# Turning x1 with VectorE block transposes and DMAs in place of TensorE transposes, in a two-layer graph kernel

## The chip, the cores and the metric

The kernel runs on one core of a Trainium2 chip. The metric is the device time of one execution in microseconds (us). Before the change the median of three runs is 2922.5 us (2921.11 to 2922.8). The profile is of one execution with a span of 2918.8 us.

Five engines work beside each other: TensorE (PE in the profile, with its weight loads as PEld), VectorE (DVE), ScalarE (ACT), GpSimd (POOL) and SyncE (SP), which here only issues DMAs. Each takes its own instructions in the order in which they stand. An instruction that has to wait for a semaphore holds up all that stand behind it on its engine.

## The reference

There are 64 graphs of 256 nodes with 512 features. The first layer is three graph convolutions with a residual and a layer norm; the second weighs a value projection with a softmax over the nodes. Cut to what matters:

```python
def gcn(x, adj, W, b):                      # per graph: [256,256] @ ([256,512] @ [512,512])
    return adj @ (x @ W) + b

h  = relu(gcn(x, adj, W1, b1))
h  = relu(gcn(h, adj, W2, b2))
x1 = layernorm(x + gcn(h, adj, W3, b3))     # "r" in the kernel

q, k = split(x1 @ Wqk)
v    = x1 @ Wv
agg  = adj @ (k * mask)
w    = mask / sqrt(512) * sum(q * agg, axis=-1)      # one score per node
out  = layernorm(x1 + softmax(w, over nodes) * v)
```

The kernel folds Wq and Wk into one matrix M once, so that the score is (x1 M) . (adj (mask x1)). All data are float32.

## The kernel before

Graphs go in pairs: 32 pairs, G = 2 graphs each. Every large product is a 2 by 2 block product by Strassen's scheme in Winograd's form: seven block products, numbered 1 to 7, in place of eight. For that, sums of blocks of both operands are made first. `a_sums` makes four sums `S` of the left operand and `b_sums` four sums `T` of the right one; `adj_sums` makes four sums `aS` of the adjacency. In the loop all three run on GpSimd.

```python
def padd(o, a, b, op=OP.add):
    nc.gpsimd.tensor_tensor(o, a, b, op=op)

def seven(mm, shape, c11, c12, c21, c22, plus=None):
    x = bank(shape); mm(1, x, True)             # left block (0,0)
    t1 = shaped(shape); nc.scalar.copy(t1, x)
    ...
    v = bank(shape); mm(7, v, True)             # needs S[2]
    mm(6, x, False)                             # needs S[1]
    u = shaped(shape); nc.scalar.copy(u, x)
    ...
    y = bank(shape); mm(2, y, True); c11(y, t1) # left block (0,1)
    mm(5, x, False)                             # needs S[0]
    q = shaped(shape); nc.scalar.copy(q, x)
    ...
    c22(v, q)                                   # reads the bank v ...
    mm(3, x, False); c12(x)                     # needs S[3]
    mm(4, v, False); c21(v, u)                  # ... that product 4 then adds to

def a_sums(hT):
    S = [pool.tile([P, 2, G, P], FP, name="S", tag="S", bufs=6) for _ in range(4)]
    blk = lambda h, k: hT[k][:, :, :, h * P:(h + 1) * P]
    padd(S[2], blk(0, 0), blk(1, 0), sub)
    padd(S[0], blk(1, 0), blk(1, 1))
    padd(S[1], S[0], blk(0, 0), sub)
    padd(S[3], blk(0, 1), S[1], sub)
    ...
```

Two generators run interleaved: `front(i)` computes the two hidden layers of pair i, and `back(i-1)` the rest of the pair before. In `back`, the third convolution ends in `r` (that is x1 before its layer norm). Then:

```python
    r = pool.tile([P, G, NH, D], FP, name="r", bufs=2)          # nodes on the partitions
    yield from adj_times(aS, C, ...)                            # writes r
    for g in range(G):
        layernorm(r[:, g])
    yield 8
    x1T = [pool.tile([P, 2, G, N], FP, name="x1T", tag="act", bufs=5) for _ in range(2)]
    for c in range(DC):                                         # features on the partitions
        pt = bank()
        for g in range(G):
            for h in range(NH):
                nc.tensor.transpose(pt[:, g, h * P:(h + 1) * P], r[:, g, h, c * P:(c + 1) * P], ident)
        nc.scalar.copy(x1T[c // 2][:, c % 2], pt)
    yield
    xm = ...                                                    # r times the mask, on ScalarE
    src = a_sums(x1T)
    ...
    def attention(g):
        v = pool.tile([P, NH, D], FP, name="v", tag="v", bufs=3)
        def mm(n, ps, first):
            for c in range(2):                                  # x1T is the stationary operand
                nc.tensor.matmul(ps, lhsT=src[n](c, g), rhs=mv[n][:, c], ...)
        ...
    yield from adj_times(aS, xmb, ...)                          # agg, into gt
    for g in range(G):
        yield from attention(g)
```

`adj_times(aS, xmb, ...)` needs r in its own layout only; `attention` needs x1T and the four sums S of it. A scheduling layer orders the instructions of the recorded program on each engine, so the order in the source isn't always that on the engine.

Of the kernel before, what the change touches and what calls it, by code (L numbers as in the profile page):

```python
# [9 lines left out]
FP = mybir.dt.float32  # L10
# [4 lines left out]
P = 128  # L15
PAIR = 2
G = PAIR
# [3 lines left out]
def gcn_then_graph_attention(ctx: ExitStack, tc: tile.TileContext, xT, xN, adjT, mask, W1, b1, W2, b2, W3, b3,  # L21
# [147 lines left out]
    mv = {}  # L169

    def make_m():

        qk = []
        for name, w in (("q", WqT), ("k", WkT)):
            qk.append([])
            for d in range(DC):
                if name == "k":
                    t = pool.tile([P, D], FP, name="wkT", tag="sup", bufs=7)
                elif d % 2 == 0:
                    two = pool.tile([P, 2, D], FP, name="wqT", tag="act", bufs=5)  # L180
                    t = two[:, 0]
                else:
                    t = two[:, 1]
                nc.sync.dma_start(t, w[d * P:(d + 1) * P, :])
                qk[-1].append(t)
        m = [pool.tile([P, 2, D], FP, name="m0", tag="v", bufs=3), const.tile([P, 2, D], FP, name="m1")]
        v0 = const.tile([P, 2, D], FP, name="v0")
        nc.sync.dma_start(v0, Wv[:HD].rearrange("(c p) f -> p c f", p=P))
        v1 = const.tile([P, 2, D], FP, name="v1")
        nc.sync.dma_start(v1, Wv[HD:].rearrange("(c p) f -> p c f", p=P))  # L190
        yield
        for f in range(DC):
            pt = bank((P, D))
            for d in range(DC):
                for j in range(DC):
                    nc.tensor.matmul(pt[:, j * P:(j + 1) * P], lhsT=qk[0][d][:, f * P:(f + 1) * P],
                                     rhs=qk[1][d][:, j * P:(j + 1) * P], start=(d == 0 and j == 0),
                                     stop=(d == DC - 1), skip_group_check=True)
            nc.scalar.copy(m[f // 2][:, f % 2, :], pt)
            yield  # L200
        ts = [const.tile([P, 2, D], FP, name=f"mv_{s}") for s in KEYS]
        b_sums((v0, m[0], v1, m[1]), ts, nc.gpsimd)
        mv.update({1: v0, 2: v1, 3: m[1], 4: ts[3], 5: ts[0], 6: ts[1], 7: ts[2]})
        yield


    def a_sums(hT):

        S = [pool.tile([P, 2, G, P], FP, name="S", tag="S", bufs=6) for _ in range(4)]
        blk = lambda h, k: hT[k][:, :, :, h * P:(h + 1) * P]  # L210
        sub = OP.subtract
        padd(S[2], blk(0, 0), blk(1, 0), sub)
        padd(S[0], blk(1, 0), blk(1, 1))
        padd(S[1], S[0], blk(0, 0), sub)
        padd(S[3], blk(0, 1), S[1], sub)
        src = {1: blk(0, 0), 2: blk(0, 1), 4: blk(1, 1), 5: S[0], 6: S[1], 7: S[2], 3: S[3]}
        return {n: (lambda c, g, t=t: t[:, c, g]) for n, t in src.items()}

    def support(hT, w):

        src = a_sums(hT)
        C = [[pool.tile([P, G, HD], FP, name="sup", tag="sup", bufs=7) for _ in range(2)] for _ in range(2)]

        def mm(n, ps, first):
            for g in range(G):
                for c in range(2):
                    nc.tensor.matmul(ps[:, g], lhsT=src[n](c, g), rhs=w[n][:, c], start=(first and g == 0 and c == 0),  # L227
                                     stop=(g == G - 1 and c == 1), skip_group_check=True)
        yield from seven(mm, (P, G, HD), lambda y, t: add(C[0][0], y, t), lambda x: nc.scalar.copy(C[0][1], x),  # L229
                         lambda v, t: add(C[1][0], v, t), lambda v, t: add(C[1][1], v, t))  # L230
        return C

    def aggregate(C, aT, b):

        hT = [pool.tile([P, 2, G, N], FP, name="hT", tag="act", bufs=5) for _ in range(2)]
        for c in range(DC):
            ps = bank()
            for g in range(G):
                for k in range(NH):
                    nc.tensor.matmul(ps[:, g], lhsT=C[k][c // 2][:, g, (c % 2) * P:(c % 2 + 1) * P],  # L240
                                     rhs=aT[:, k, g], start=(g == 0 and k == 0), stop=(g == G - 1 and k == NH - 1),
                                     skip_group_check=True)
            nc.scalar.activation(hT[c // 2][:, c % 2], ps, AF.Relu, bias=b[:, c:c + 1])  # L243
            yield
        return hT
# [36 lines left out]
    def layernorm(t):  # L282
        mvt, rs = stats(t)
        for h in range(NH):
            nc.vector.tensor_scalar(t[:, h, :], t[:, h, :], mvt[:, h, 0:1], rs[:, h:h + 1],  # L285
                                    op0=OP.subtract, op1=OP.mult)
# [34 lines left out]
    def back(i, hT, aT, prev):  # L321
        x = load_x(i)
        if prev is not None:
            sm = softmax_rows(prev[2])
        src = support(hT, wl[2])
        for _ in range(3):
            next(src)
# [3 lines that stand above are left out]
                padd(x[:, g, h, :], x[:, g, h, :], b3b)  # L331
        if prev is not None:
            s = softmax_cols(sm)
            for g in range(G):
                finish(i - 1, g, prev, s)
        C = yield from src
        aS = adj_sums(aT)
        r = pool.tile([P, G, NH, D], FP, name="r", bufs=2)
        xb = lambda h, j: x[:, :, h, j * HD:(j + 1) * HD]
        rb = lambda h, j: r[:, :, h, j * HD:(j + 1) * HD]  # L340
        yield from adj_times(aS, C, lambda y, t: add(rb(0, 0), y, t), lambda x: add(rb(0, 1), x, xb(0, 1)),
                             lambda v, t: add(rb(1, 0), v, t), lambda v, t: add(rb(1, 1), v, t),
                             plus=(xb(0, 0), xb(1, 0), xb(1, 1)))
        for g in range(G):
            layernorm(r[:, g])
        yield 8
        x1T = [pool.tile([P, 2, G, N], FP, name="x1T", tag="act", bufs=5) for _ in range(2)]
        for c in range(DC):
            pt = bank()
            for g in range(G):  # L350
                for h in range(NH):
                    nc.tensor.transpose(pt[:, g, h * P:(h + 1) * P], r[:, g, h, c * P:(c + 1) * P], ident)
            nc.scalar.copy(x1T[c // 2][:, c % 2], pt)
        yield
        xm = pool.tile([P, G, NH, D], FP, name="xm", tag="x", bufs=1)
        for h in range(NH):
            for g in range(G):
                b = i * G + g
                nc.scalar.activation(xm[:, g, h, :], r[:, g, h, :], AF.Copy, scale=mask_t[:, h, b:b + 1])  # L359
        xmb = [[xm[:, :, h, j * HD:(j + 1) * HD] for j in range(2)] for h in range(2)]  # L360
        src = a_sums(x1T)
        gt = pool.tile([P, NH, G, D], FP, name="gt", bufs=1)
        gb = lambda h, j: gt[:, h, :, j * HD:(j + 1) * HD]
        w = small.tile([P, NH, G], FP, name="w", bufs=2)
        vs = [None] * G

        def attention(g):
            b = i * G + g
            v = pool.tile([P, NH, D], FP, name="v", tag="v", bufs=3)

            def mm(n, ps, first):
                for c in range(2):
                    nc.tensor.matmul(ps, lhsT=src[n](c, g), rhs=mv[n][:, c], start=(first and c == 0),  # L373
                                     stop=(c == 1), skip_group_check=True)

            def score(y, h):
                prod = tmp()
                nc.vector.scalar_tensor_tensor(prod, y, mask_s[:, h, b:b + 1], gt[:, h, g, :], op0=OP.mult,
                                               op1=OP.mult, accum_out=w[:, h, g:g + 1])

            def c22(ps, t):
                y = tmp()
                add(y, ps, t)
                score(y, 1)
            vs[g] = v
            yield from seven(mm, (P, D), lambda y, t: add(v[:, 0, :], y, t), lambda x: score(x, 0),
                             lambda ps, t: add(v[:, 1, :], ps, t), c22)
        yield from adj_times(aS, xmb, lambda y, t: add(gb(0, 0), y, t), lambda x: nc.scalar.copy(gb(0, 1), x),
                             lambda v, t: add(gb(1, 0), v, t), lambda v, t: add(gb(1, 1), v, t))
        for g in range(G):  # L390
            yield from attention(g)
        return r, vs, w
# [79 lines left out]
```

## Time and profile before

| what | value |
|---|---|
| median of three runs | 2922.5 us |
| granted TensorE clock, mean | 0.997 |
| one pair in the steady state (transposes of the first pair begin at 124.9 us, of the last at 2867.9 us, 31 steps between them) | 88.5 us |
| TensorE transposes of x1, per pair | 16, in 4 PSUM banks |
| ScalarE copies of them to x1T, per pair | 4, 601 ns each |
| DMAs in the steady state, per pair | 5: xT, x, adjacency in; two halves out |
| mean DMA rate over the span | 43 GB/s |

In rows of the profile, `L352` is a line of the kernel, the engine and operation follow, then the tiles written and read with buffer numbers left out (`ps` is a PSUM bank), the shape and the count; behind the bar stand the busy time of the group and the mean duration of one, then the idle time of the engine just before them and who ended it. A float32 matrix product appears as two matmul instructions, each with a weight load, so the counts of L227, L240, L265 and L373 are twice those in the source; the transposes appear once. Rows of the timeline have the start in us from the start of the span, the duration of the merged stretch, the engine, the line and the operation, with the count last.

### The profile page before, as it was taken

What the parts mean: (1) busy time and instruction counts of PE and PEld (TensorE: products, weight loads), DVE (VectorE), ACT (ScalarE), POOL (GpSimd) and SP (SyncE); (2) the same over time, 40 slices, a digit from 0 to 9 for tenths busy, and PEclk for the clock granted to TensorE, in tenths of its full rate; (3) what the DMA queues carried; (4) which work ended last, traced back from release to release, by engine and by line L of the source; (5) the groups of instructions that cost most, each with busy time, mean ns of one, the idle gap of its engine ahead of it and who ended that gap; (6) DMA issues with size and microseconds to landing.
All of it is one profiled execution on the core that took longest, in us unless ns stands there. A gap on an engine that the chain in (4) does not pass through costs nothing. (4 is left out here: it accounts for less than half of the span.)

```text
span 2918.8 us, 30346 instructions
## 1 busy us (share of the span) xinstructions
PE 2883.0 (99%) x11776; PEld 2150.7 (74%) x11776; DVE 1009.2 (35%) x2126; ACT 911.4 (31%) x1574; POOL 1346.4 (46%) x1130
## 2 busy tenths in 40 slices
PE   8999999999999999999999999999999999999996
PEld 7787777877777777778777787777787777877773
DVE  2233323333333333233333333332333333333325
ACT  2332333323333323333223333233332323332332
POOL 5534445444455344544444543545444445435442
PEclk9999999999999999999999999999999999999999
DMA  4101101111011011010110110110101101101000
GB/s 149 37 29 51 51 22 51 42 39 51 22 51 51 29 51 45 28 51 32 48 51 22 51 51 29 51 38 35 51 29 51 51 22 51 51 29 51 37 15 29
DMA packets 28719, 126.01 MB, mean 43 GB/s; under 512 B 3232, under 2 KB 6432, under 8 KB 20384
## 3 DMA queue, kind: packets, MB, share of 16 engines
q1 hardware_dynamic: 28576, 124.08, 11.7%
q8 instruction: 93, 1.52, 0.2%
q14 instruction: 50, 0.41, 0.0%
HBM read 90.51 MB, written 33.55 MB: 43 GB/s over the span
## 5 line engine op out<-in xcount | busy, mean ns | idle before, releaser
L227 PE MATMUL ps<-w_T,S 128*128 128x256 f32 x2304 | 524.0, 379 | 2.2 <-DVE w_T L85 1.6
L227 PEld LDWEIGHTS ps<-w_T,S 128*128 128x128 f32 x2304 | 437.5, 190 | 63.1 <-POOL S L61 2.7
L240 PE MATMUL ps<-aT,sup 128*128 128x256 f32 x2048 | 484.0, 381 | 0.0
L240 PEld LDWEIGHTS ps<-aT,sup 128*128 128x128 f32 x2048 | 386.4, 190 | 61.8 <-DVE sup L58 10.6
L373 PE MATMUL ps<-mv_T,S 128*128 128x512 f32 x768 | 350.5, 592 | 0.0
L58 DVE TENSOR_TENSOR sup<-ps,tmp 128x512 f32<-128x512 f32 x288 | 194.1, 683 | 441.1 <-PE ps L227 396.8
L243 ACT ACTIVATE hT<-ps,b 128x512 f32<-128x512 f32 x256 | 176.0, 688 | 441.6 <-PE ps L240 441.6
L111 ACT COPY tmp<-ps 128x512 f32<-128x512 f32 x224 | 131.3, 586 | 523.9 <-PE ps L227 290.8
L373 PEld LDWEIGHTS ps<-mv_T,S 128*128 128x128 f32 x768 | 145.9, 190 | 183.7 <-issue 168.6
L102 ACT COPY tmp<-ps 128x512 f32<-128x512 f32 x224 | 130.2, 581 | 401.4 <-PE ps L227 212.0
L119 ACT COPY tmp<-ps 128x512 f32<-128x512 f32 x224 | 130.7, 584 | 399.1 <-PE ps L373 180.5
L373 PE MATMUL ps<-v,x1T 128*128 128x512 f32 x512 | 251.0, 592 | 0.0
L227 PE MATMUL ps<-w,hT 128*128 128x256 f32 x1024 | 245.2, 382 | 0.0
L83 POOL TENSOR_TENSOR T<-sup 128x512 f32<-128x512 f32 x32 | 40.7, 1271 | 436.3 <-ACT sup L229 436.3
L61 POOL TENSOR_TENSOR S<-hT 128x512 f32<-128x512 f32 x128 | 162.5, 1270 | 144.7 <-PE ps L373 104.7
L58 DVE TENSOR_TENSOR v<-ps,tmp 128x512 f32<-128x512 f32 x128 | 88.5, 691 | 405.5 <-PE ps L373 405.5
L58 DVE TENSOR_TENSOR gt<-ps,tmp 128x512 f32<-128x512 f32 x96 | 66.4, 692 | 414.2 <-PE ps L265 388.6
L227 PEld LDWEIGHTS ps<-w,hT 128*128 128x128 f32 x1024 | 189.6, 190 | 24.5
L58 DVE TENSOR_TENSOR r<-ps,tmp 128x512 f32<-128x512 f32 x96 | 65.3, 680 | 407.6 <-PE ps L265 270.5
L265 PE MATMUL ps<-T,aS 128*128 128x256 f32 x768 | 197.0, 386 | 3.5 <-POOL T L85 3.5
L227 PE MATMUL ps<-w,S 128*128 128x256 f32 x768 | 179.1, 382 | 1.5 <-ACT tmp L119 0.8
L83 POOL TENSOR_TENSOR T<-xm 128x512 f32<-128x512 f32 x32 | 40.8, 1274 | 285.4 <-ACT xm L359 277.5
(94 smaller groups left out, 4059.0 us busy)
## 6 DMA issues: line engine op xcount, KB each, us to landing
xT<-in_xT SPq DMA_DIRECT2D x32, 1024.0 KB, 4.7
x<-in_xN SPq DMA_DIRECT2D x32, 1024.0 KB, 4.8
out<-v SPq DMA_DIRECT2D x64, 512.0 KB, 2.6
aT<-in_adjT SPq DMA_DIRECT2D x32, 512.0 KB, 5.4
w<-in_W SPq DMA_DIRECT2D x9, 256.0 KB, 5.2
wqT<-in_WqT SPq DMA_DIRECT2D x4, 256.0 KB, 5.2
wkT<-in_WkT SPq DMA_DIRECT2D x4, 256.0 KB, 5.0
v<-in_Wv SPq DMA_DIRECT2D x2, 512.0 KB, 6.4
```

The costliest lines, as they stand in the source:

```text
L58: nc.vector.tensor_tensor(o, a, b, op=OP.add)
L61: nc.gpsimd.tensor_tensor(o, a, b, op=op)
L83: eng.tensor_tensor(Ts[0], B[1], B[0], op=sub)
L102: nc.scalar.copy(t1, x)
L111: nc.scalar.copy(u, x)
L119: nc.scalar.copy(q, x)
L227: nc.tensor.matmul(ps[:, g], lhsT=src[n](c, g), rhs=w[n][:, c], start=(first and g == 0 and c == 0), stop=(g == G - 1 and c == 1), skip_gr ...
L240: nc.tensor.matmul(ps[:, g], lhsT=C[k][c // 2][:, g, (c % 2) * P:(c % 2 + 1) * P], rhs=aT[:, k, g], start=(g == 0 and k == 0), stop=(g == ...
L243: nc.scalar.activation(hT[c // 2][:, c % 2], ps, AF.Relu, bias=b[:, c:c + 1])
L265: nc.tensor.matmul(ps[:, g], lhsT=aS[n][:, g], rhs=mov[n][:, g], start=(first and g == 0), stop=(g == G - 1), skip_group_check=True)
L373: nc.tensor.matmul(ps, lhsT=src[n](c, g), rhs=mv[n][:, c], start=(first and c == 0), stop=(c == 1), skip_group_check=True)
```

## The change

x1 is no longer turned on TensorE. VectorE transposes blocks of 32 by 32 in place of it, into a new tile `tr`; a block stays in its group of 32 partitions. Sixteen DMAs per pair then move the blocks between the four partition groups, into x1T. So that each run of a DMA is 512 bytes, x1T has a new layout: the two chunks c and the two graphs g lie innermost, and the weight loads of `attention` step over every fourth element. The block sums keep reading whole contiguous rows. The aim is to take this work off TensorE and PSUM. x1T has a buffer of its own now, so the pool `act` goes from 5 to 4 buffers; to make room for `tr`, `r` goes from 2 to 1 and `v` from 3 to 2.

```diff
-    def a_sums(hT):
-        S = [pool.tile([P, 2, G, P], FP, name="S", tag="S", bufs=6) for _ in range(4)]
-        blk = lambda h, k: hT[k][:, :, :, h * P:(h + 1) * P]
+    def a_sums(blk, shape):
+        S = [pool.tile(list(shape), FP, name="S", tag="S", bufs=6) for _ in range(4)]
 ...
-        hT = [pool.tile([P, 2, G, N], FP, name="hT", tag="act", bufs=5) for _ in range(2)]
+        hT = [pool.tile([P, 2, G, N], FP, name="hT", tag="act", bufs=4) for _ in range(2)]
 ...
-        r = pool.tile([P, G, NH, D], FP, name="r", bufs=2)
+        r = pool.tile([P, G, NH, D], FP, name="r", bufs=1)
 ...
+        tr = pool.tile([P, 4, NH, 2, 32, 2, G], FP, name="tr", bufs=1)
+        x1T = pool.tile([P, NH, 2, P, 2, G], FP, name="x1T", bufs=1)
         for g in range(G):
             layernorm(r[:, g])
+            for h in range(NH):
+                for k in range(2):
+                    nc.vector.transpose(tr[:, :, h, k, :, :, g].rearrange("p q j c -> p c q j"),
+                                        r[:, g, h, k * HD:(k + 1) * HD].rearrange("p (c q j) -> p c q j", c=2, q=4))
+        for q in range(4):
+            for a in range(4):
+                nc.sync.dma_start(x1T[q * 32:(q + 1) * 32, :, :, a * 32:(a + 1) * 32].rearrange("p h k j c g -> p (h k) (j c g)"),
+                                  tr[a * 32:(a + 1) * 32, q].rearrange("p h k j c g -> p (h k) (j c g)"))
         yield 8
-        x1T = [pool.tile([P, 2, G, N], FP, name="x1T", tag="act", bufs=5) for _ in range(2)]
-        for c in range(DC):
-            pt = bank()
-            for g in range(G):
-                for h in range(NH):
-                    nc.tensor.transpose(pt[:, g, h * P:(h + 1) * P], r[:, g, h, c * P:(c + 1) * P], ident)
-            nc.scalar.copy(x1T[c // 2][:, c % 2], pt)
-        yield
         xm = ...
-        src = a_sums(x1T)
+        src = a_sums(lambda h, k: x1T[:, h, k], (P, P, 2, G))
 ...
-            v = pool.tile([P, NH, D], FP, name="v", tag="v", bufs=3)
+            v = pool.tile([P, NH, D], FP, name="v", tag="v", bufs=2)
             def mm(n, ps, first):
                 for c in range(2):
-                    nc.tensor.matmul(ps, lhsT=src[n](c, g), rhs=mv[n][:, c], ...
+                    nc.tensor.matmul(ps, lhsT=src[n][:, :, c, g], rhs=mv[n][:, c], ...
```

More of the change, by code (lines that the diff above doesn't have):

```diff
@@ L179, in make_m @@
                 elif d % 2 == 0:
-                    two = pool.tile([P, 2, D], FP, name="wqT", tag="act", bufs=5)
+                    two = pool.tile([P, 2, D], FP, name="wqT", tag="act", bufs=4)
                     t = two[:, 0]
@@ L185, in make_m @@
                 qk[-1].append(t)
-        m = [pool.tile([P, 2, D], FP, name="m0", tag="v", bufs=3), const.tile([P, 2, D], FP, name="m1")]
+        m = [pool.tile([P, 2, D], FP, name="m0", tag="v", bufs=2), const.tile([P, 2, D], FP, name="m1")]
         v0 = const.tile([P, 2, D], FP, name="v0")
@@ L215, in a_sums @@
         padd(S[3], blk(0, 1), S[1], sub)
-        src = {1: blk(0, 0), 2: blk(0, 1), 4: blk(1, 1), 5: S[0], 6: S[1], 7: S[2], 3: S[3]}
-        return {n: (lambda c, g, t=t: t[:, c, g]) for n, t in src.items()}
+        return {1: blk(0, 0), 2: blk(0, 1), 4: blk(1, 1), 5: S[0], 6: S[1], 7: S[2], 3: S[3]}
     def support(hT, w):
-        src = a_sums(hT)
+        src = a_sums(lambda h, k: hT[k][:, :, :, h * P:(h + 1) * P], (P, 2, G, P))
         C = [[pool.tile([P, G, HD], FP, name="sup", tag="sup", bufs=7) for _ in range(2)] for _ in range(2)]
@@ L226, in mm @@
                 for c in range(2):
-                    nc.tensor.matmul(ps[:, g], lhsT=src[n](c, g), rhs=w[n][:, c], start=(first and g == 0 and c == 0),
+                    nc.tensor.matmul(ps[:, g], lhsT=src[n][:, c, g], rhs=w[n][:, c], start=(first and g == 0 and c == 0),
                                      stop=(g == G - 1 and c == 1), skip_group_check=True)
@@ L368, in attention @@
             b = i * G + g
-            v = pool.tile([P, NH, D], FP, name="v", tag="v", bufs=3)
+            v = pool.tile([P, NH, D], FP, name="v", tag="v", bufs=2)
             def mm(n, ps, first):
                 for c in range(2):
-                    nc.tensor.matmul(ps, lhsT=src[n](c, g), rhs=mv[n][:, c], start=(first and c == 0),
+                    nc.tensor.matmul(ps, lhsT=src[n][:, :, c, g], rhs=mv[n][:, c], start=(first and c == 0),
                                      stop=(c == 1), skip_group_check=True)
```

## The prediction

> **What bounds the kernel now.** I read the engine totals first, then the table by stages, then the timeline of one pair.
>
> ```profile
> PE 2883.0 (99%) x11776; PEld 2150.7 (74%) x11776; DVE 1009.2 (35%) x2126; ACT 911.4 (31%) x1574; POOL 1346.4 (46%) x1130
> ```
>
> ```profile
> 654.00:742.50 88.50, 88.50 (x361) 65.91 (x361) 31.05 (x66) 27.43 (x48) 41.14 (x35) 1.00 0.12 42
> ```
>
> The second line is one pair in the steady state: 88.50 us long, PE busy for all 88.50, then weight loads, DVE, ACT and POOL, clock 1.00. TensorE sets the pace and hardly waits, so a PE instruction taken away is worth its full length, but only if nothing that PE needs comes later than it does now. The timeline of the pair around the transposes decides that:
>
> ```profile
> 740.87 0.67 DVE L58 TENSOR_TENSOR sup<-ps,tmp 128x512 f32<-128x512 f32 x1
> ...
> 742.53 1.89 PE L227 MATMUL ps<-w_T,hT 128*128 128x256 f32 x8
> ...
> 744.26 6.39 PE L240 MATMUL ps<-aT,sup 128*128 128x256 f32 x28
> 744.46 0.69 DVE L58 TENSOR_TENSOR sup<-ps,tmp 128x512 f32<-128x512 f32 x1 [2.01 <-PE ps L227]
> ...
> 750.49 1.91 PE L352 MATMUL ps<-ident,r 128*128 128x128 f32 x16
> ...
> 752.24 1.03 PE L265 MATMUL ps<-xm,aT 128*128 128x256 f32 x4
> 752.42 2.50 POOL L61 TENSOR_TENSOR S<-x1T 128x512 f32<-128x512 f32 x2 [4.51 <-ACT x1T L353]
> ...
> 758.52 1.03 PE L265 MATMUL ps<-T,aT 128*128 128x256 f32 x4
> ...
> 759.39 1.02 PE L373 MATMUL ps<-v,x1T 128*128 128x512 f32 x2
> ...
> 760.02 1.41 POOL L61 TENSOR_TENSOR aS<-aT 128x256 f32<-128x256 f32 x2
> 760.25 3.60 PE L373 MATMUL ps<-mv_T,S 128*128 128x512 f32 x8
> ```
>
> To see here: the transposes take from 750.49 to 752.24; GpSimd starts the sums of x1T at 752.42, nearly 8 us before PE reads the first of them (760.25); the sums aS of the next adjacency come after them, at 760.02, where nobody is in a hurry. The two DVE additions at 740.87 and 744.46 are results of the second hidden layer that PE is about to need.
>
> **What the Trainium skill says.** (1) "VectorE: DVE Perf Modes", section "The three transpose paths": VectorE turns blocks of 32 by 32 only and writes to SBUF. The kernel before has none, so no duration is to be had from its trace. (2) "SBUF — State Buffer", section "Specifications (TRN2)": lines of 16 bytes, with full bandwidth only from two hits per line. The new weight loads step 16 bytes, one hit per line; no weight load before has a step, so this is open. (3) "TensorE: Matmul & The Clock Gate", section "Step-by-step: what each phase is for": a weight load is pulled ahead of running matmuls. The trace agrees: for the 512-column products of L373 a load takes 190 ns while matmuls follow each other every 428 ns (eight from 760.25 to 763.68). (4) "SBUF — State Buffer", section "The DMA setup-cost knee": about 2 us fixed for a DMA. The stores of the output (512 KB) land 2.6 us after issue.
>
> **The change part by part**, per pair, on the clock of the timeline above. Where I say how instructions stand, I read the built program of the changed kernel, engine by engine, with what each waits for.
>
> *A. Removed from PE:* 16 transposes, 752.24 - 750.49 = 1.75 us (0.109 each), over 32 pairs 56 us or 1.9%. The four ACT copies of 0.60 us go too, off the path.
>
> *B. Added on DVE:* 8 block transposes of 128x256. From this trace: BATCH_NORM_STATS2 on 512 elements takes 0.685 us and a second follows after 0.60; the 256-element operations L294 and L301 take 0.41 and 0.34. I estimate 0.35 us each back to back, 1.4 us for four. Four stand after the normalisation of graph 0 and so ahead of the addition now at 740.87; it then ends at 743.0 in place of 741.54. Product 4 of the support (742.53) adds to the PSUM bank which that addition reads, and starts at about 743.05: 0.5 us later. The other four stand ahead of the addition now at 744.46: normalisation of graph 1 until 743.95, transposes until 745.35, addition until 746.05. PE finishes product 4 at 744.8 and has six matmuls (1.3 us) to do before it needs that sum, until 746.1: just in time. PE now loses some 0.1 to 0.2 us there, so the net is +0.4 us.
>
> *C. Added DMAs:* 16 of 64 KB, issued by SP once all transposes are done (745.4). An issue takes 0.34 to 0.47 us (at the start of the kernel four follow in 2.50 us, with waits for queue slots). I take 0.47: the last is issued at 752.5 and lands 2.6 later, at about 755. PE wants x1T for product 1 of attention at 750.9 + 28 matmuls x 0.216 = 757.0. So the DMAs are hidden, with 2 us to spare.
>
> *D. Moved on POOL:* in the changed program the four aS sums stand ahead of the sums of x1T, and the first aS waits until PE has finished the last product that reads the old aS (the xm,aS group), the last but one of `adj_times`, about 0.6 us before that ends at 757.0 with the wait's own delay counted. So aS runs from 756.4 to 759.35 (four, 2.95 us as at 760.02 to 762.9 now), S[2] until 760.6, S[0] 761.9, S[1] 763.1. PE ends product 1 at 758.7 and waits 1.9 us for S[2] (product 7), 1.7 us for work, then 0.75 us for S[1] (product 6). After that it has what it needs. Together +2.65 us, whatever the DMAs do, as long as they land before 759.
>
> *E. Weight loads with a step:* they cost nothing up to 428 ns.
>
> *F. Fewer buffers:* r is read last at 710.8 (the residual of the pair before) and written next at 728.85; v is stored at 713.24, has landed by 716, and is written next at 765.65. The act pool no longer holds x1T. No new wait.
>
> *Sum:* -1.75 + 0.4 + 2.65 = +1.3 us per pair, times 31 is +40 us. In the last pair nothing overlaps: four transposes stand ahead of graph 1's normalisation there, some 2 us more. 2922.5 + 42 = 2965. The unknowns B, C and E can only add, so I go to 2972.
>
> **The rivals.** *R1, all is hidden:* if D failed (the aS sums running early, or S in time), PE would keep most of A: 2922.5 - 56 + 31 x 0.4 = about 2880. For it: PE is the bound and every other engine is less than half busy. Against: the aS wait is in the program, and the idle time of POOL is of no use to a queue that stands. *R2, slow DMAs:* if SP needs 1 us for each, the last lands at 745.5 + 15 + 2.6 = 763, S[2] comes at 764.4 in place of 760.6, 3.8 us more per pair: about 3080. For it: the waits for queue slots; against: the issues seen. *R3, slow block transposes:* at 0.6 us each the first addition ends 1 us later still and the second at 748.2, and PE, out of other work at 747.2, stands: +2 us per pair, about 3030. For it: writes with a 16-byte step on a form never seen here. *R4, weight loads above 428 ns:* each 100 ns over costs 1792 x 0.1 = 179 us. Against: 190 would have to grow by 2.3.
>
> **Range and chances.** R1 in part, one in eight; plain sum, one in two; R2 or R3 in part, one in three; R4, one in sixteen. That gives 2915 to 3050 for eight in ten. Faster by over 2% (below 2864) needs all of A and more: 0.04. Slower by over 2% begins at 2981, only 9 us above my figure: 0.45. Within: 0.51.
>
> **What the profile after would show.** A: no L352 rows and some 56 us less matmul time. B: transposes of about 0.4 us, and PE starting product 4 of the second support about 0.5 us after product 3 ends. C: x1T landing 9 to 10 us after the last transpose. D: PE idle at the first mv_T,S products of each pair, released by POOL, about 2.6 us per pair, 80 us in all, with aS ahead of S on POOL. E: loads of x1T at 190 to 400 ns. F: no wait of DVE for a store of v. I am wrong if PE waits at product 1 for a DMA, or at the sup sums for DVE, for more than half a us per pair, or if the stepped loads show above 428 ns.

## The result and the profile after

The changed kernel takes **3037.4 us** (median of four runs, 3035.37 to 3039.57) against 2922.0 us in the same session: the ratio is 1.0395, with a 95% interval of 1.0377 to 1.0413. It is slower by 115 us, more than twice the 49.5 us forecast.

The engine totals of the changed kernel's page, and the window from one load of xT to the next (span of time; then busy us of PE, PEld, DVE, ACT and POOL, clock, DMA share, GB/s):

```profile
PE 2882.2 (95%) x11264; PEld 2300.5 (76%) x11264; DVE 1134.6 (37%) x2382; ACT 849.3 (28%) x1446; POOL 1358.3 (45%) x1130
```

```profile
740.94:833.77 92.83, 89.19 (x350) 71.33 (x349) 35.01 (x75) 26.35 (x45) 42.07 (x36) 1.00 0.17 51
```

PE has 512 instructions fewer and is still busy for as long as before, with 5% of the span idle in place of 1%. From one load of xT to the next a pair takes 92.84 us in the steady state; the same distance before is 89.37. (The 88.5 us named above for the kernel before is a mean over 31 steps from transposes to transposes, and the last step, with no next pair beside it, is much shorter. Steady pairs are 89.37 apart: their transposes begin at 661.12 and 750.49, for example.) That is **+3.46 us per pair**, 104 us over some 30 pairs. The rest is mostly the last stretch, which takes 13 us longer: from the last load of x to the end 117.4 in place of 104.4.

The groups of instructions whose idle time grew (last columns: idle us ahead of them in the whole run, and who ended it):

```profile
L374 PE MATMUL ps<-mv_T,S 128*128 128x512 f32 x768 | 370.3, 612 | 63.0 <-POOL S L61 63.0
...
L226 PE MATMUL ps<-w_T,hT 128*128 128x256 f32 x512 | 124.2, 385 | 22.5 <-DVE sup L58 22.5
...
L61 POOL TENSOR_TENSOR aS<-aT 128x256 f32<-128x256 f32 x64 | 46.1, 739 | 263.0 <-PE ps L264 263.0
L264 PE MATMUL ps<-xm,aS 128*128 128x256 f32 x128 | 36.2, 405 | 21.6 <-ACT tmp L119 21.6
```

In the kernel before, the three groups of PE had no wait:

```profile
L373 PE MATMUL ps<-mv_T,S 128*128 128x512 f32 x768 | 350.5, 592 | 0.0
L227 PE MATMUL ps<-w_T,hT 128*128 128x256 f32 x512 | 120.9, 379 | 0.0
L265 PE MATMUL ps<-xm,aS 128*128 128x256 f32 x128 | 35.6, 400 | 0.0
```

A group that follows a wait is also recorded as longer (370.3 in place of 350.5 us for `mv_T,S`, with as many instructions), which is the larger part of why the busy time of PE did not fall with the transposes. Three waits of PE are new: for GpSimd (63.0), for VectorE (22.5) and for a copy of ScalarE (21.6). The first two were in the prediction, the third was not. The row of POOL shows what GpSimd waits for itself: the first aS of a pair stands 8.5 us (263.0 over 31) until PE has read the old one.

The timeline of one pair around these waits (start, length, the engine's row; in brackets the idle time ahead of it and who ended it):

```profile
764.14 2.04 DVE L349 STREAM_TRANSPOSE tr<-r 128x256 f32<-128x256 f32 x4
766.05 0.67 DVE L58 TENSOR_TENSOR sup<-ps,tmp 128x512 f32<-128x512 f32 x1
766.77 1.99 PE L226 MATMUL ps<-w_T,hT 128*128 128x256 f32 x8 [0.72 <-DVE sup L58]
...
769.64 10.42 SPq L353 DMA_DIRECT2D x1T<-tr  x16
780.35 1.13 PE L264 MATMUL ps<-xm,aS 128*128 128x256 f32 x4 [0.68 <-ACT tmp L119]
781.32 1.03 PE L264 MATMUL ps<-T,aT 128*128 128x256 f32 x4
781.57 1.41 POOL L61 TENSOR_TENSOR aS<-aT 128x256 f32<-128x256 f32 x2 [8.48 <-PE ps L264]
782.18 1.89 PE L374 MATMUL ps<-v,x1T 128*128 128x512 f32 x4
784.42 2.49 POOL L61 TENSOR_TENSOR S<-x1T 128x512 f32<-128x512 f32 x2
785.74 2.11 PE L374 MATMUL ps<-mv_T,S 128*128 128x512 f32 x4 [1.66 <-POOL S L61]
788.30 2.11 PE L374 MATMUL ps<-mv_T,S 128*128 128x512 f32 x4 [0.46 <-POOL S L61]
```

To see here: four transposes push the sup addition to 766.05, and PE stands 0.72 us for it. The sixteen DMAs take SP 10.4 us; a landing takes 2.1 us, so x1T is there at about 781.7. At 781.57 GpSimd starts with aS, and only at 784.42 with S, for which PE stands twice. All four matmuls of `v,x1T`, the first product of attention, stand behind the last adjacency product (`T,aT`). In the kernel before, two of them stood ahead of `xm,aS`, whose turn had not come because ScalarE was still copying:

```profile
756.72 1.02 PE L373 MATMUL ps<-v,x1T 128*128 128x512 f32 x2
757.58 1.11 PE L265 MATMUL ps<-xm,aS 128*128 128x256 f32 x4
```

Work that covers a wait in this way is called filler below.

Laid beside the timeline of before, instruction by instruction, the loss per pair is this (a negative number is a gain):

| Where | us per pair |
|---|---|
| transposes gone from PE | -1.75 |
| waits for the two sup additions behind transposes | +1.19 |
| wait for ScalarE's copy in the adjacency products, where a product of attention stood as filler before | +0.86 |
| waits for S behind aS on GpSimd | +2.91 |
| the rest of attention, with longer weight loads | +0.25 |
| sum | +3.46 |

These are readings of two traces, and a wait taken away may only uncover the next one. The experiments test them.

### The profile page after: what moved, and what is told of

It is laid out like the page before. It is cut to its first block, busy times and chain, and to the rows that moved or that the text cites. A ratio compares the mean times of both kernels' runs of the same rounds, so it can differ in the third digit from the quotient of the medians.

```text
span 3034.3 us, 30378 instructions
## 1 busy us (share of the span) xinstructions
PE 2882.2 (95%) x11264; PEld 2300.5 (76%) x11264; DVE 1134.6 (37%) x2382; ACT 849.3 (28%) x1446; POOL 1358.3 (45%) x1130
## 5 line engine op out<-in xcount | busy, mean ns | idle before, releaser
L374 PE MATMUL ps<-mv_T,S 128*128 128x512 f32 x768 | 370.3, 612 | 63.0 <-POOL S L61 63.0
L374 PEld LDWEIGHTS ps<-mv_T,S 128*128 128x128 f32 x768 | 232.3, 310 | 186.1 <-POOL S L61 107.0
L374 PEld LDWEIGHTS ps<-v,x1T 128*128 128x128 f32 x512 | 155.5, 310 | 59.6 <-issue 3.3
```

The lines of the kernel that those rows point to most:

```text
L374: nc.tensor.matmul(ps, lhsT=src[n][:, :, c, g], rhs=mv[n][:, c], start=(first and c == 0), stop=(c == 1), skip_group_check=True)
```

## Experiments

A period below is the distance of two loads of xT in the steady state, as above, averaged over 24 pairs; each ratio is against the kernel before, run beside it.

**1. GpSimd's order.** The sums aS are queued behind S of x1T again, nothing else:

```diff
-        aS = adj_sums(aT)
+        with (tc.issue_after(last["x1"]) if "x1" in last else nullcontext()):   # the last S of x1T
+            aS = adj_sums(aT)
```

> The changed kernel with one thing put back: on GpSimd the four sums aS of the next adjacency are queued behind the sums S of x1T, as in the kernel before. Theory (GpSimd's order costs some 2.9 us per pair): PE's idle time at the first mv_T,S products of a pair (1.66 + 0.46 us, released by POOL) goes, 2.1 to 2.9 us per pair, 65 to 90 us in all: 2950 to 2970 us. Rival (it is the late x1T that GpSimd waits for, its order is harmless): the same wait is then released by the DMAs of x1T, PE still stands about 1.5 us or more per pair: above 3010 us.

Measured: 2956.3 us (1.0124, 1.0109 to 1.0139), a period of 90.20. The two PE groups in it:

```profile
L377 PE MATMUL ps<-mv_T,S 128*128 128x512 f32 x768 | 356.6, 598 | 0.5
...
L227 PE MATMUL ps<-w_T,hT 128*128 128x256 f32 x512 | 124.2, 385 | 22.3 <-DVE sup L58 22.3
```

The wait of 63.0 is 0.5, that for VectorE is untouched: 81 us, or 2.64 per pair, belong to GpSimd's order. The rival is out: the DMAs of x1T are the same in this kernel, and PE no longer waits there.

**2. VectorE's order.** The transposes go behind the sup addition that product 4 waits for, four of them still ahead of the other one:

```diff
         yield 8
+        for g in range(G):
+            with tc.issue_after(last["c22" if g == 0 else "c21"]):   # the sup sums
+                (the four transposes of g)
+        (the 16 DMAs)
```

> The changed kernel with the block transposes moved on VectorE only: the sum for product 4 of the second support (sup, lower right) goes ahead of all of them, and the other sup sum stands behind four and not eight. Theory (the transposes cost PE 1.2 us per pair by holding up these two sums): 0.9 to 1.2 us per pair less, 3000 to 3010 us, with PE's idle 0.72 us at product 4 gone. Rival (the transposes delay x1T, the sums have time enough): no gain or a loss, 3035 us or more, with new waits at the first product of attention for the DMAs.

Measured: 3000.4 us (1.0277, 1.0262 to 1.0293), a period of 91.75.

```profile
L380 PE MATMUL ps<-mv_T,S 128*128 128x512 f32 x768 | 368.2, 609 | 13.9 <-POOL S L61 13.2
L380 PE MATMUL ps<-v,x1T 128*128 128x512 f32 x512 | 256.0, 613 | 48.0 <-DMA x1T<-tr 41.9 <-issue 6.1
```

The number is the theory's, but both sides were right in part. The wait at product 4 is gone. In its place PE waits 48.0 us ahead of the products with x1T, 41.9 of them for the DMAs, which the later transposes delay, and that time is taken out of the wait for GpSimd, which the aS sums would have imposed anyway. The DMAs were hidden with hardly any slack.

**3. The new layout of x1T in the kernel before.** PE transposes as before, x1T written by ScalarE with the 16-byte step, the buffers cut as in the change:

```diff
-            nc.scalar.copy(x1T[c // 2][:, c % 2], pt)
+            for h in range(NH):
+                nc.scalar.copy(x1T[:, h, c // 2, :, c % 2, :].rearrange("p n g -> p g n"),
+                               pt[:, :, h * P:(h + 1) * P])
```

> The kernel before with its PE transposes, but x1T written by ScalarE in the new layout (weights read with a 16-byte step) and the buffers cut as in the changed kernel (r 1, v 2, act 4). No block transposes, no DMAs between partitions. Theory (loads take 308 in place of 190 ns and hide under 428 ns of matmul; the buffers cost nothing): within 0.3% of the kernel before, at most 0.25 us per pair, 2918 to 2931 us. Rival (stepped weight loads or stepped GpSimd reads are a good part of the loss): 1 us per pair or more, 2950 us and above.

Measured: 2979.7 us (1.0205, 1.0189 to 1.0220). The rival's number, but not its reason:

```profile
L263 PE MATMUL ps<-T,aS 128*128 128x256 f32 x768 | 202.9, 387 | 48.9 <-ACT tmp L102 45.8 <-POOL T L85 3.1
...
L352 ACT COPY x1T<-ps 128x256 f32<-128x256 f32 x256 | 123.2, 681 | 0.0
```

PE waits 45.8 us for ScalarE, which now makes eight copies of 681 ns per pair (5.4 us) where it made four of 601, and the products after this wait take 5.9 us longer (202.9 against 197.0). So this run says nothing against the loads: it has a cost of its own. Of the 59 us some 7 are left; the products m,S take 8.0 us longer (133.3 against 125.3 us), and no other group of attention grew by more than 1 us.

**4. No exchange.** The transposes write straight into x1T, the 16 DMAs are left out (so the blocks stay in their partition group and attention works on other numbers); the built program has the order of the kernel before on PE and GpSimd.

```diff
-        for q in range(4):
-            for a in range(4):
-                nc.sync.dma_start(x1T[...], tr[...])
+        # x1T is tr
```

> The changed kernel without the 16 DMAs between partition groups: the block transposes write straight into x1T, so the blocks stay in their own partition group (left out: the exchange; the numbers of attention differ). In the built program PE and GpSimd then have the order of the kernel before: a product of attention stands as filler in the adjacency products, aS behind S. Theory (per pair: 1.75 gained from PE's transposes, 1.2 lost to the two late sums, 0.25 to loads and waits, nothing else): -0.3 us per pair, 2905 to 2925 us, so order and DMAs together account for all of the slowdown. Rival (the block transposes on VectorE are the main cost): 2960 us or more.

Measured: 2917.6 us (0.9989, 0.9982 to 0.9995), a period of 89.08, which is 0.29 less than before. The sum -1.75 + 1.19 + 0.25 holds. Without the exchange neither GpSimd's wait nor the one for ScalarE's copy appears. This run also has the cut buffers, so they cost nothing that shows.

**5. Transposes that write without a step.** The DMAs move the same bytes from the same places, but the blocks land elsewhere, so attention again works on other numbers:

```diff
-   nc.vector.transpose(tr[:, :, h, k, :, :, g].rearrange("p q j c -> p c q j"), r[...].rearrange(...))
+   nc.vector.transpose(tr_flat[:, 256 * ((2 * g + h) * 2 + k):][:, :256], r[:, g, h, k * HD:(k + 1) * HD])
```

> The changed kernel with one thing altered: the eight block transposes write 256 floats in a row and not with a 16-byte step (the DMAs move the same bytes, so the blocks land in other places and the numbers of attention differ; nothing is left out). Theory A (the stepped write is what makes a transpose take 0.63 us, 0.5 us apart): 0.35 us each and less, four in 1.4 us, PE's idle time at product 4 of the second support falls from 0.72 to about 0.1 us, some 20 us less in all: 3015 us. Theory B (a block transpose of fp32 costs this whatever it writes): the same 0.6 us each and 3037 us.

Measured: 2914.0 us (0.9977, 0.9968 to 0.9986), a period of 89.00.

```profile
L226 PE MATMUL ps<-w_T,hT 128*128 128x256 f32 x512 | 124.2, 385 | 5.6 <-DVE sup L58 5.6
L349 DVE STREAM_TRANSPOSE tr<-r 128x256 f32<-128x256 f32 x256 | 90.6, 410 | 0.0
```

One transpose takes 410 ns where the changed kernel's take 632, and four take 1.41 us in place of 2.04: the step was the cost. The total fell by far more than theory A said, because in this build GpSimd has three of the four sums S of x1T ahead of every aS. So it has to be set against run 1, which has all four ahead: 42 us, 1.20 per pair. By groups, 16.7 us come from product 4's wait (22.3 to 5.6), 12 from the aggregation `aT,sup`, which waits for the other sup sum (486.4 + 4.0 to 478.1), and 12 from attention, whose x1T lands sooner.

**6. Runs 1 and 2 together.**

```diff
+            with tc.issue_after(last["x1"]) ...:     # aS, as in run 1
+            with tc.issue_after(last["c22" if g == 0 else "c21"]):     # transposes, as in run 2
```

> The changed kernel with GpSimd's order put back and the block transposes moved behind the sup sum, both at once. Theory (once GpSimd and VectorE are out of the way the 16 transfers on one queue are the next wait): PE's wait for VectorE (22 us) goes, but a wait for the DMAs of x1T of 40 to 50 us stands in its place, 1.3 us or more per pair: 2955 to 2980 us, no better than GpSimd's order alone (2956). Rival (the gains add up, 2956 - 37): 2920 us.

Measured: 2981.2 us (1.0214, 1.0197 to 1.0231), a little above the theory's range. PE waits 50.2 us ahead of `v,x1T`, 44.1 of them for the DMAs. With GpSimd out of the way, the later transposes cost more than the earlier sup sum gains: the version is worse than run 1 alone.

**7. Two queues.** Run 1, and

```diff
-                nc.sync.dma_start(x1T[...], tr[...])
+                (nc.sync if (q + a) % 2 == 0 else nc.scalar).dma_start(x1T[...], tr[...])
```

> The changed kernel with GpSimd's order put back and the 16 DMAs given in turn to two queues, SP's and ScalarE's. In the built program the first product of attention then stands again among the adjacency products. Theory (x1T is there 4 to 5 us sooner, the filler covers the wait for ScalarE's tmp copy of 21.6 us in all): 2925 to 2940 us. Rival (ScalarE spends 8 x 0.6 us on issuing and its copies to hT and tmp come late): 2956 us or more, with PE waiting for ScalarE.

Measured: 2917.1 us (0.9989, 0.9981 to 0.9998), below the theory's range, and a period of 89.13, 1.07 less than in run 1.

```profile
L227 PE MATMUL ps<-w_T,hT 128*128 128x256 f32 x512 | 124.2, 385 | 22.5 <-DVE sup L58 22.5
L265 PE MATMUL ps<-xm,aS 128*128 128x256 f32 x128 | 35.0, 396 | 0.0
```

With the filler back the 21.6 us ahead of `xm,aS` are gone; the wait for VectorE is still whole. ScalarE's issues did no harm here.

**8. Runs 1, 2 and 7 together.**

```diff
+            with tc.issue_after(last["x1"]) ...:     # run 1
+            with tc.issue_after(last["c22" if g == 0 else "c21"]):     # run 2
+                (nc.sync if (q + a) % 2 == 0 else nc.scalar).dma_start(...)     # run 7
```

> GpSimd's order put back, the block transposes behind the sup sum, and the DMAs in turn on two queues. Theory (the four waits of the changed kernel are all removed and TensorE keeps most of the 1.75 us of its transposes): 2890 to 2915 us, faster than the kernel before by 0.3 to 1%. Rival (ScalarE's issues hold up its own copies, which PE needs): 2930 us or more, with PE waiting for ScalarE.

Measured: 2943.9 us (1.0082, 1.0067 to 1.0097). The rival is right:

```profile
L268 PE MATMUL ps<-T,aS 128*128 128x256 f32 x768 | 206.0, 392 | 53.3 <-ACT tmp L102 49.0 <-POOL T L85 2.2 <-POOL T L84 1.6
```

The issues on ScalarE's queue wait for the transposes. With the transposes late they stand between its copies of hT, and its copy tmp comes after them, while PE waits. In run 7 the eight issues came before those copies.

**9. No step anywhere.** The transposes write rows of 32 values, x1T is laid out so that weights are read in a row, GpSimd's order is put back; a DMA now moves pieces of 128 bytes:

```diff
-        tr = pool.tile([P, 4, NH, 2, 32, 2, G], FP, name="tr", bufs=1)
-        x1T = pool.tile([P, NH, 2, P, 2, G], FP, name="x1T", bufs=1)
+        tr = pool.tile([P, 4, G, NH, 2, 2, 32], FP, name="tr", bufs=1)
+        x1T = pool.tile([P, G, NH, 2, 2, P], FP, name="x1T", bufs=1)
```

> The full computation with the block transposes writing rows of 32 floats side by side, x1T laid out so that weights are read without a step, and GpSimd's order put back; the 16 DMAs stay on one queue, but now move 16 pieces of 128 bytes per partition in place of 4 of 512. Theory (the step of 16 bytes was the cost, in the transposes as in the loads; a DMA costs its 0.6 us of issue and 2.1 us of landing whatever its pieces): 2905 to 2912 us, the no-step time of 2914 less 0.25 us per pair for loads of 190 ns again. Rival (four times as many pieces make the DMAs slower, x1T comes late): 2930 us or more, with PE or GpSimd waiting for x1T's DMAs.

Measured: 2921.1 us (1.0003, 0.9994 to 1.0012), between the theory's time and the rival's. The loads take 190 ns and `m,S` 125.3 us again, but an issue takes 627 ns at the median in place of 599 and a landing 2.2 us. PE's products `mv_T,S`, which need the sums of x1T, take 357.6 us and wait 2.6, in run 5 350.5 and 0.0.

**10. The same on two queues**, here without the `issue_after` of run 1:

```diff
-                nc.sync.dma_start(x1T[...], tr[...])
+                (nc.sync if (q + a) % 2 == 0 else nc.scalar).dma_start(x1T[...], tr[...])
```

> As the run before it, with the DMAs in turn on SP's and ScalarE's queue; in the built program GpSimd's order is that of the kernel before without a hint, and the first product of attention stands among the adjacency products again. Theory (all four costs are gone: order, slow transposes, lost filler, stepped loads; TensorE keeps most of its 1.75 us): 2875 to 2895 us. Rival (pieces of 128 bytes are slow, or ScalarE's issues delay its copies): 2915 us or more.

Measured: 2978.7 us (2971.11 to 2988.98; 1.0201, 1.0177 to 1.0226). The line of x1T in the trace (issue to landing, shortest, median, longest), and PE's row:

```profile
DMA to landing us min/median/max: 2.2/3.9/5.1
```

```profile
L374 PE MATMUL ps<-v,x1T 128*128 128x512 f32 x512 | 265.8, 622 | 64.4 <-DMA x1T<-tr 64.4
```

The rival's first reason holds. Here the small pieces cost: 3.9 us to land, against 2.6 in run 7 with 512 bytes on two queues. The filler product wants x1T earlier than it comes and holds up PE's queue.

**11. A step of 8 bytes.** Only the two chunks c stand side by side; pieces of 256 bytes; one queue; GpSimd's order put back:

```diff
+        tr = pool.tile([P, 4, G, NH, 2, 32, 2], FP, name="tr", bufs=1)
+        x1T = pool.tile([P, G, NH, 2, P, 2], FP, name="x1T", bufs=1)
```

> The full computation with a step of 8 bytes in place of 16: only the two column halves c stand side by side, the graph g is an outer index; the DMAs move 8 pieces of 256 bytes per partition; one queue, GpSimd's order put back. Theory (what costs is one value per 16 bytes, and at two values the transposes take 0.41 us and the loads 190 ns again; the DMAs stay at 0.60 us of issue and 2.1 us of landing): 2903 to 2914 us. Rival (any step costs): transposes near 0.5 to 0.63 us, loads of 250 to 308 ns, and 2920 to 2956 us.

Measured: 2913.7 us (0.9975, 0.9966 to 0.9985), a period of 88.94.

```profile
L351 DVE STREAM_TRANSPOSE tr<-r 128x256 f32<-128x256 f32 x256 | 90.7, 412 | 0.0
L377 PEld LDWEIGHTS ps<-mv_T,x1T 128*128 128x128 f32 x256 | 50.2, 196 | 59.7 <-issue 59.5 <-DVE tmp L382 0.2
```

Both costs of the step are gone at 8 bytes: 412 ns and 196 ns, and a landing takes 2.1 us.

**12. The same on two queues**, with the filler:

```diff
-                nc.sync.dma_start(x1T[...], tr[...])
+                (nc.sync if (q + a) % 2 == 0 else nc.scalar).dma_start(x1T[...], tr[...])
```

> As the run before it with the DMAs in turn on SP's and ScalarE's queue; in the built program the first product of attention stands among the adjacency products again and wants x1T some 3 us earlier. Theory (pieces of 256 bytes land as those of 512 do on two queues, 2.6 us, and not in the 3.9 us of 128 bytes): 2880 to 2900 us, faster than the kernel before by about 1%. Rival (they land late as the 128-byte pieces on two queues did): 2925 us or more, with PE waiting for x1T's DMAs.

Measured: **2896.3 us** (0.9914, 0.9897 to 0.9930), a period of 88.45: faster than both kernels, with the full computation.

```profile
L377 PE MATMUL ps<-v,x1T 128*128 128x512 f32 x512 | 253.8, 598 | 11.6 <-DMA x1T<-tr 6.4 <-PE ps L265 4.6
L227 PE MATMUL ps<-w_T,hT 128*128 128x256 f32 x512 | 124.2, 386 | 5.8 <-DVE sup L58 5.8
...
L265 PE MATMUL ps<-xm,aS 128*128 128x256 f32 x128 | 35.5, 400 | 0.0
```

A period of 89.37 - 1.75 = 87.62 would keep all of the transposes' time; this version keeps about half of it. A landing takes 3.1 us at the median here, and the filler waits a little for it.

## Why the prediction was wrong

The direction was right, the size was not: +1.3 us per pair was forecast, +3.46 came, and the last stretch cost 13 us more where 2 were forecast. By its steps:

- **A, right in size.** The transposes gave back the 1.75 us: the period of run 4 comes out with it. The sign that was named for it, some 56 us less matmul time, did not come (PE is busy 2882.2 us, before 2883.0), mostly because the groups that follow a wait are recorded as longer; in run 12, with few waits, PE is busy 2838.1 us.
- **B, mis-sized: 0.4 against 1.19.** Two things failed. The duration: 0.35 us apart was taken from other VectorE operations, and four took 2.04 us and not 1.4. Run 5 shows why: the estimate fits a transpose that writes in a row (four in 1.41 us) and misses the 16-byte step. Rival R3 named this and shared a third of the chances with R2. That its 3030 us lie near 3037.4 is luck: it put 2 us more per pair on this step, and 0.79 came. And the second sup sum, called "just in time", was not: run 5 gives back 0.4 us per pair at the aggregation that needs it (half of this the kernel before lost too: 484.0 us there, 478.1 in run 5). PE's wait of 0.72 us per pair for VectorE is one of the signs of being wrong that the prediction named.
- **C, right in outcome, wrong in its slack.** No issue took 0.47 us; 0.60 did, so x1T was there some 12 us after the last transpose and not 9 to 10, within half a us of PE's need and not 2 us ahead. Runs 2 and 6 show the price: what delays the transposes delays PE.
- **D, right in mechanism and nearly in size.** 2.65 was forecast, 2.91 read from the traces, and 2.64 per pair measured by run 1. This is the largest part of the loss, 81 of 115 us.
- **The step that was missing: 0.86.** The text took "28 matmuls x 0.216" for the adjacency products, PE going through without a stop. In the kernel before, a product of attention stood among them while ScalarE made a copy. It needs x1T, and in the changed program it stands after them. PE then waits 0.68 us for the copy. Run 7 brings the filler back and the wait is 0.0. The prediction took GpSimd's new order from the built program, but not this change of PE's.
- **E, nearly right.** The loads rose from 190 to about 308 ns and hide under 428, except in `m,S`: 8 us in all, 0.25 per pair. Runs 9 and 11 have 125.3 and 125.8 us there, without the 16-byte step.
- **F, right.** No wait for the buffers, in the changed kernel or in run 4.

So run 1 (2.64), run 5 against run 1 (1.20), the filler (0.86, read from the traces; run 7 gained 1.07 over run 1 with the filler and the second queue together) and the loads (0.25), less the 1.75, make 3.20; product 4's rest of a wait for VectorE in run 5 (5.6 us, 0.18 per pair) makes 3.38 of the 3.46.

The last stretch was not tried by itself, and its cause stays open in part. It begins with the attention of the pair before, so that pair's waits for S (1.05 and 0.46 us) are in it. Of the last pair itself the traces show this, first before, then after the change:

```profile
2867.92 3.79 PE L352 MATMUL ps<-ident,r 128*128 128x128 f32 x16 [3.98 <-DVE r L285]
2873.84 1.99 PE L265 MATMUL ps<-T,aS 128*128 128x256 f32 x8 [1.26 <-POOL T L85]
```

```profile
2978.11 1.22 PE L264 MATMUL ps<-xm,aT 128*128 128x256 f32 x2 [1.71 <-ACT xm L360]
2980.85 4.15 PE L264 MATMUL ps<-T,aS 128*128 128x256 f32 x8 [1.53 <-POOL T L84]
2991.68 3.07 PE L374 MATMUL ps<-v,x1T 128*128 128x512 f32 x4 [1.83 <-DMA x1T<-tr]
```

PE stands for the masked copy of graph 1, whose normalisation comes after four transposes. The same eight matmuls `T,aS` then take 4.15 us where they took 1.99: the granted clock is 0.50 from 2975.0 to 2985.0; before, it was 0.71 from 2867.9 to 2873.8 and 1.00 from there to 2881.0. Only after this does PE wait 1.83 us for x1T. The exchange is not the main part: run 4, which has none, takes 111.9 us from its last load of x to the end, 7.5 more than before, with a clock of 0.61 from 2861.5 to 2879.4. The prediction counted only the four transposes, 2 us. The range ended at 3050, so the measured time lies inside it; the central figure failed by B, by the missing filler and by the last stretch.

"SBUF — State Buffer", section "Specifications (TRN2)", of the Trainium skill says that lines have 16 bytes and full bandwidth needs two hits per line. The runs agree, nearly in full at two hits: at one float per 16 bytes a load takes 308 ns and a transpose 632, at two floats 196 and 412, in a row 190 and 410. "DMA: Bandwidth & Descriptors" gives 512 bytes as the least transfer for line rate (section "Specifications"), but says that transfers from SBUF to SBUF, as these are, do not suffer from small descriptors (section "Why small descriptors are slow (HBM only)"). On one queue the runs nearly agree with the latter (2.1, 2.1 and 2.2 us to land at 512, 256 and 128 bytes); on two queues they do not (2.6, 3.1 and 3.9), and no run shows why.

It also stays open why the built program puts aS ahead of S in one version and behind it in another; that the order follows small changes of layout or queue is all that the runs show. Nor was a version tried in which the transposes of the last pair are placed by hand.

## What to carry to other kernels

An operation taken off the busiest engine is worth its time only if nothing that this engine needs comes later: compare each engine's order in the built program before and after, and look for work that stood as filler inside a wait, not only for new waits. When a layout is chosen to suit a DMA, price its step in every instruction that writes or reads it; a step of two floats with pieces of half the size was here better than either extreme. A transfer that is hidden with only half a us to spare becomes a wait as soon as its start is put off, as in runs 2 and 6.

## What was not expected of the hardware

- A float32 block transpose of 128x256 takes 632 ns with a 16-byte step of its output and 410 without; four follow each other in 2.04 and 1.41 us.
- A weight load of 128x128 float32 takes 308 ns with a 16-byte step, 196 with 8 bytes and 190 in a row.
- A DMA of 64 KB from SBUF to SBUF costs its queue 0.60 us of issue, more than the 1 MB load of x (0.34 to 0.37), so sixteen small ones fill 10.4 us of SP.
- ScalarE copies from PSUM into a layout with a 16-byte step at 681 ns per 256 columns, against 601 ns for 512 columns in a row.
